# A mixture of experts behind a long convolution: routed gate and up products counted in half feature tiles

## The chip, the cores and the metric

The kernel runs on one core of a Trainium2 chip. The metric is the time of one execution on the device in microseconds (us). A core has TensorE (PE: matmuls, with its weight loads shown apart as PEld), VectorE (DVE), ScalarE (ACT), GpSimd (POOL), the SyncE queue (SP) that issues transfers, and 16 DMA engines.

## The reference

128 sequences with 32 heads of 512 features each (4096 rows of 512, called tokens here) go through a causal long convolution with a per-head kernel, are cut to each sequence's length, and then pass a mixture of experts; the result is added to the input.

```
y = irfft(rfft(x, 1024) * rfft(K, 1024))[..., :512] + x * D
y = y * (arange(512) < length[:, None])[:, None, :]     # lengths from 78 to 453

scores = sigmoid(y @ gate_w.T) + bias                   # 16 experts
w, idx = top_k(scores, 4);  w = w / sum(w)
for each expert e:   g = y @ Wg[e].T;  u = y @ Wu[e].T  # 512 -> 256
                     out += (w[e] * silu(g) * u) @ Wd[e].T
out += silu(y @ Sg.T) * (y @ Su.T) @ Sd.T               # shared expert
return x + out
```

What matters here: behind a sequence's length, features are zero. A token of a sequence of length 200 needs only its first 200 features in the products with gate_w, Wg and Wu.

## The kernel before

All data are float32. The work has three stretches. In the first (to about 145 us) TensorE convolves head by head (`convolve`, L515 to L535): matmuls against a strip of shifted kernels, then transposes that also sort the sequences by falling length, so that features stand on partitions and tokens on columns (`yT`, in the large tile `store`). Features are reversed, so that the zero features of short sequences come first: a token that needs n tiles of 128 features uses the last n of KT = 4. Convolved rows also go to a buffer in device memory, `y_rows`, with their routing weights behind them.

In the second stretch (about 145 to 298 us) `unit_step` computes the shared expert for 8 units of 16 sequences, while `slots` plans the routed work in steps between them. Each expert's tokens, sorted by falling length, fill tiles of 128 slots; the plan holds for each tile its expert (`texp`), the place of its weights in a ring (`woff`), the number of feature tiles that its longest token needs (`ntk`, 1 to 4, from the flags `reach` at L464), the rows to fetch (`get`) and the rows to add to (`put`).

The third stretch (about 298 to 925 us) goes over the routed tiles in an order written out by hand. `turn_of(step)` (L1121) is one turn of a software pipeline over three tiles at once; instructions keep this order on each engine:

- `gather(step + 4)`: GpSimd fetches the rows of a later tile into `yg`.
- `tokens(step)` (L1016): TensorE transposes the needed feature tiles (L1022, PSUM tile `m`), ScalarE copies them to `yt` (L1028), DVE picks each token's weight (L1029).
- `turn(step - 2)` (L1070): TensorE transposes the hidden values `zt` of an older tile in two halves (L1072, PSUM tile `u`), DVE copies them to `zT` (L1075).
- `inner(step - 1)` (L1050): for each needed feature tile one product of 128 rows with 512 columns, gates in the first 256 columns and ups in the rest, into one PSUM bank `g` (L1054). Then ScalarE's Silu (L1065) and DVE's product with the ups and the weight (L1066) make `zt`.
- `outer(step - 2)` (L1077): two products of 512 columns give the output (L1080, PSUM tile `o`); DVE copies it to `ob` (L1089), GpSimd adds it to the rows in device memory (L1090).
- `registers(step + 1)` (L1044): TensorE's instruction stream loads two values of the plan, the weights' place and the number of feature tiles (L1045, L1048).
- SyncE loads an expert's weights into the ring when the tile begins a new expert (L1139 to L1146).

The number of feature tiles is known only on the chip. `by_tiles` (L901) therefore compiles four versions of a piece of code and chooses by two comparisons on TensorE's stream. It is used for the transposes (L1027), for `inner` (L1063) and for the shared expert's products (L937).

The ring has R = 8 places of WSZ = 3072 columns (gates and ups 2048, down 1024; 1.5 MB each) and is loaded R - 1 experts ahead. It lies over `yT`, which the units release one after the other (`free_after`, L964). The last turns (L1153 on) each first ask for a flag whether there is such a tile.

Of the kernel before, what the change touches and what calls it, by code (L numbers as in the profile page):

```python
# [31 lines left out]
I32 = mybir.dt.int32  # L32
# [8 lines left out]
E, TOPK, I = 16, 4, 256  # L41
KT = L // P
IT = I // P
HB = 4
# [7 lines left out]
YW = L + E  # L52
R = 8
SPARE = 16
# [4 lines left out]
QC = P // KT  # L59
WSZ = 2 * KT * I + IT * L  # L60

# [14 lines left out]
def ssm_moe_kernel(  # L76
# [41 lines left out]
    for j in range(2):  # L118
# [19 lines left out]

    store = big.tile([P, 3 * WSZ + KT * H * P], F32, tag="store", name="store")
    yT = store[:, 2 * WSZ : 2 * WSZ + KT * H * P].rearrange(  # L140
        "p (u k h b) -> p u k h b", u=NU, k=KT, h=H
    )
    w_sh = store[:, 2 * WSZ + KT * H * P :]
    ring_flat = store[:, : R * WSZ]
    y_rows = d1.tile([B * H, YW], F32, tag="y_rows", name="y_rows")
# [73 lines left out]
    less = const.tile([E, P], BF16, tag="less", name="less")  # L219
    nc.gpsimd.memset(less, -float(KT - 1))  # L220

# [241 lines left out]

    reach = const.tile([P, KT], BF16, tag="reach", name="reach")  # L464
    nc.vector.memset(reach, 1.0)
    for n in range(1, KT):
        nc.vector.tensor_scalar(
            reach[:, n : n + 1], by_rank[:, 1:2], float(n * P), None, ALU.is_gt
        )
# [174 lines left out]
    def slots():  # L644
# [6 lines left out]

        pe = ps_m.tile([E, KT], F32, tag="m", name="pe")
        nc.tensor.matmul(pe, lhsT=cnt, rhs=reach, start=True, stop=True)
        many = ctile("many", [E, KT])
        nc.vector.tensor_copy(many, pe)
# [21 lines left out]
        t_e = tpos[:E, :]  # L677
        marks = ctile("marks", [E, KT + 1, NT], BF16)
        upto_n = ctile("upto_n", [E, KT - 1])
        nc.vector.tensor_scalar(  # L680
            upto_n, many[:, 1:], 1.0 / P, tstart, ALU.mult, ALU.add
        )
        nc.vector.tensor_scalar(marks[:, 0, :], t_e, tend, None, ALU.is_ge)
        nc.vector.tensor_scalar(marks[:, KT, :], t_e, tstart, None, ALU.is_lt)
        for n in range(1, KT):
            nc.vector.tensor_scalar(
                marks[:, n, :], t_e, upto_n[:, n - 1 : n], None, ALU.is_lt
            )
# [8 lines left out]
        nc.tensor.matmul(pr[:, 1, :], lhsT=used_b, rhs=marks[:, 0, :], start=True, stop=True)  # L697
        for n in range(1, KT):
            nc.tensor.matmul(
                pr[:, 2, :], lhsT=ones[:E, :], rhs=marks[:, n, :], start=(n == 1), stop=False  # L700
            )
        nc.tensor.matmul(pr[:, 2, :], lhsT=less, rhs=marks[:, KT, :], start=False, stop=True)
        rows3 = ctile("rows3", [P, 3, NT])
# [46 lines left out]
        def mod_r(dst, src, add):  # L750
# [8 lines left out]
        place, first = trow("place"), trow("first")  # L759
        woff, loff, load = trow("woff", I32), trow("loff", I32), trow("load", I32)  # L760
        mod_r(place, num[:1, :], 0)
        nc.vector.tensor_scalar(woff, place, float(WSZ), None, ALU.mult)
        mod_r(place, num[:1, :], R - 1)
        nc.vector.tensor_scalar(loff, place, float(WSZ), None, ALU.mult)
# [10 lines left out]
        made.update(  # L775
            texp=texp, woff=woff, load=load, loff=loff, lexp=lexp, lexp0=lexp0, ntk=ntk, fresh=fresh, full=full
        )
# [67 lines left out]
    xb = load_xt(0)  # L845
    nc.sync.dma_start(out=w_sh, in_=w_all[E])

# [52 lines left out]

    def by_tiles(k_t, some):  # L901


        with tc.If(k_t > 2) as many:
            with tc.If(k_t > 3) as all4:
                some(4)
            with all4.Else():
                some(3)
        with many.Else():
            with tc.If(k_t > 1) as two:  # L910
                some(2)
            with two.Else():
                some(1)

# [49 lines left out]
    def free_after(j):  # L964

        return min((max(j - 1, 0) * WSZ - 1) // (KT * TU), NU - 1)

# [3 lines left out]
    def unit_step(u):  # L971
# [3 lines left out]
        if u < NU:  # L975
            k_us[u] = nc.tensor.value_load(k_u[0:1, u : u + 1], min_val=1, max_val=KT)
            for it in range(IT):
                up(u, it, p_g, 0)
                if u == 0 and it == 0:
                    sums(NB - 1)  # L980
                    route(NB // RB - 1)
                nc.scalar.activation(sgu[it], p_g[it], AF.Silu)
                up(u, it, p_u, I)
                nc.vector.tensor_mul(at(zu, u)[:, it, :], sgu[it], p_u[it])
                if u > 0 or it > 0:
                    next(making, None)
# [15 lines left out]

    w0s, k_ts = {}, {}

    yt = homes(gp, "yt", [P, KT, P], 2)
    wts = homes(gp, "wt", [P, 1], 4)
    junks = homes(gp, "junk", [P, E], 2)
    sgs = homes(gp, "sgt", [P, I], 2)
    zs = homes(gp, "zt", [P, I], 2)
    zts = homes(gp, "zT", [P, IT, P], 2)  # L1010
    p_t, p_gu = homes(ps_m, "m", [P, KT, P], 2), homes(ps_g, "g", [P, 2 * I], 2)
    p_z = homes(ps_u, "u", [P, IT, P], 2)

    marks = {}

    def tokens(t):  # L1016
# [9 lines left out]
        else:  # L1026
            by_tiles(k_ts[t], transposes)  # L1027
        nc.scalar.copy(at(yt, t), pt)  # L1028
        nc.vector.scalar_tensor_tensor(  # L1029
            at(junks, t),  # L1030
# [7 lines left out]

    def in_ring(t, mm):
        for other in loads[t + 1 :]:  # L1040
            tc.declare_no_dep(mm.ins, other.ins, reason="another place of the ring")
        dep(mm, loads[t], "the tile's expert")

    def registers(t):  # L1044
        w0s[t] = nc.tensor.value_load(  # L1045
            made["woff"][0:1, t : t + 1], min_val=0, max_val=(R - 1) * WSZ
        )
        k_ts[t] = nc.tensor.value_load(made["ntk"][0:1, t : t + 1], min_val=1, max_val=KT)  # L1048

    def inner(t):  # L1050
        pgu = at(p_gu, t)
        def products(n):
            for q in range(KT - n, KT):
                mm = nc.tensor.matmul(  # L1054
                    pgu,
                    lhsT=at(yt, t)[:, q, :],
                    rhs=ring_flat[:, bass.ds(w0s[t] + q * 2 * I, 2 * I)],
                    start=(q == KT - n),
                    stop=(q == KT - 1),
                )  # L1060
                in_ring(t, mm)

        by_tiles(k_ts[t], products)  # L1063
        sg = at(sgs, t)
        nc.scalar.activation(sg, pgu[:, :I], AF.Silu)  # L1065
        nc.vector.scalar_tensor_tensor(  # L1066
            at(zs, t), pgu[:, I:], at(wts, t), sg, ALU.mult, ALU.mult
        )

    def turn(t):  # L1070
        for it in range(IT):
            nc.tensor.transpose(  # L1072
                at(p_z, t)[:, it, :], at(zs, t)[:, it * P : (it + 1) * P], ident
            )
        nc.vector.tensor_copy(at(zts, t), at(p_z, t))  # L1075

# [90 lines left out]
def _laid_out(inputs):  # L1167
# [9 lines left out]
    )  # L1177
    wgu = np.concatenate([wg, wu], axis=3).reshape(rows, P, KT * 2 * I)
    wd = wd.reshape(rows, L, IT, P).transpose(0, 3, 2, 1).reshape(rows, P, IT * L)
    laid = {  # L1180
# [10 lines left out]
        "bias": a["L0_ffn_bias"],  # L1191
        "w_all": np.concatenate([wgu, wd], axis=2),
    }
# [22 lines left out]
```

## Time and profile before

| what | value |
|---|---|
| runs of the kernel | 941.65, 943.94, 944.29 us; median 943.94 |
| the profiled execution: its time, its span | 942.44 us, 940.7 us |
| granted clock of TensorE over the span | 0.994 |
| stretch of the routed tiles, 298 to 923 us | 625.0 us, PE busy 621.6, DVE 222.2, ACT 130.3, POOL 343.1 |
| L1054, gate and up products | 742 records, busy 343.0 us |
| L1080, down products | 536 records, busy 252.2 us |
| L1022 and L1072, transposes | 373 and 268 records, busy 63.1 and 51.2 us |
| L1028, copy of the transposes (ACT, 128x512) | 136 of 586 ns |
| L1065, Silu (ACT, 128x256) | 135 of 384 ns |
| L1066, product to zt (DVE, 128x256) | 135 of 484 ns |
| L1075, copy to zT (DVE, 128x256) | 134 of 420 ns |

A group's row gives line, engine and operation, what it writes and reads, the count, then busy time in us and the mean length of one in ns, then the idle time of the engine just before such instructions, and what ended it. TensorE's matmuls overlap: the length of one runs from its start to its modelled end, and the next begins before that. What a matmul takes from the engine is read from the distances between starts. A float32 matmul appears as two records, each with its own weight load. A row of the timeline gives start and length in us, engine, line, operation, tiles and count. The view of one source line gives count and shortest/median/longest ns; an engine's name with a q stands for its instruction stream (register loads, branches, waits), which is not counted as busy. A row of busy times by stretch gives the stretch, its length, then busy time and number of instructions of PE, PEld, DVE, ACT and POOL, the granted clock, the busy share of the DMA engines and GB/s.

### The profile page before, as it was taken

What the parts mean: (1) busy time and instruction counts of PE and PEld (TensorE: products, weight loads), DVE (VectorE), ACT (ScalarE), POOL (GpSimd) and SP (SyncE); (2) the same over time, 40 slices, a digit from 0 to 9 for tenths busy, and PEclk for the clock granted to TensorE, in tenths of its full rate; (3) what the DMA queues carried; (4) which work ended last, traced back from release to release, by engine and by line L of the source; (5) the groups of instructions that cost most, each with busy time, mean ns of one, the idle gap of its engine ahead of it and who ended that gap; (6) DMA issues with size and microseconds to landing.
All of it is one profiled execution on the core that took longest, in us unless ns stands there. A gap on an engine that the chain in (4) does not pass through costs nothing.

```text
span 940.7 us, 14509 instructions
## 1 busy us (share of the span) xinstructions
PE 883.1 (94%) x2960; PEld 442.0 (47%) x2960; DVE 409.3 (44%) x1406; ACT 190.0 (20%) x375; POOL 422.7 (45%) x376
## 2 busy tenths in 40 slices
PE   0799997999999999999999999999999999999993
PEld 0455553444544444454444444444444444444441
DVE  7954555486950233433343334333433233344331
ACT  0122221111222122211222122212211111222220
POOL 4210000222456455655565456645655545566553
PEclk9999999999999999999999999999999999999997
DMA  4378873276769756776577567756766556667664
GB/s 163 108 253 290 293 275 137 30 249 132 184 96 233 198 111 115 138 170 116 110 135 181 114 115 126 130 101 110 134 113 114 100 106 109 109 130 138 118 114 83
DMA packets 54673, 135.95 MB, mean 145 GB/s; under 512 B 12400, under 2 KB 12560, under 8 KB 50960
## 3 DMA queue, kind: packets, MB, share of 16 engines
q0 software_dynamic: 36256, 89.77, 50.6%
q1 hardware_dynamic: 14064, 36.15, 11.3%
q10 hardware_dynamic: 4224, 8.39, 2.3%
q8 instruction: 71, 1.16, 0.5%
q14 instruction: 58, 0.48, 0.1%
HBM read 288.08 MB, written 60.64 MB: 371 GB/s over the span
## 4 chain that ended last, share of the span: by engine, by line
PE 66%; issue 1%; SPq 0%; POOL 0%; DVE 0%; ACT 0%; POOLq 0%
PE g L1054 34%; PE o L1080 24%; PE m L1022 4%; PE u L1072 3%; PE o L944 1%; POOL out L1090 0%; SPq L1157 0%; POOL yg L894 0%; SPq L1105 0%; SPq L1140 0%; SPq L1141 0%; DVE zt L1066 0%; SPq L1142 0%; ACT sgt L1065 0%; SPq L880 0%
## 5 line engine op out<-in xcount | busy, mean ns | idle before, releaser
L1054 PE MATMUL g<-store,yt 128*128 x742 | 343.0, 596 | 1.8 <-issue 1.5
L1090 POOL DMA_INDIRECT out<-ob,put x134 | 211.3, 1577 | 242.6 <-DVE junk L1029 214.4
L1080 PE MATMUL o<-store,zT 128*128 x536 | 252.2, 593 | 0.1
L1066 DVE SCALAR_TENSOR_TENSOR zt<-g,wt,sgt 128x256 f32<-128x256 f32 x135 | 65.3, 484 | 306.7 <-ACT sgt L1065 306.7
L1054 PEld LDWEIGHTS g<-store,yt 128*128 128x128 f32 x742 | 130.3, 190 | 118.7 <-issue 117.4
L1080 PEld LDWEIGHTS o<-store,zT 128*128 128x128 f32 x536 | 101.4, 190 | 129.3 <-issue 124.6
L894 POOL DMA_INDIRECT yg<-y_rows,get x140 | 138.1, 987 | 42.7 <-issue 31.7
L1089 DVE COPY ob<-o 128x512 f32<-128x512 f32 x134 | 92.7, 692 | 109.7 <-PE o L1080 101.6
L1028 ACT COPY yt<-m 128x512 f32<-128x512 f32 x136 | 79.7, 586 | 227.7 <-PE m L1022 219.3
L1065 ACT ACTIVATE sgt<-g 128x256 f32<-128x256 f32 x135 | 51.9, 384 | 268.2 <-PE g L1054 267.4
L953 POOL DMA_INDIRECT out<-ob,unit_rows x32 | 50.2, 1568 | 98.8 <-ACT ob L951 93.1
L520 PE MATMUL py<-strip,xt 128*128 128x512 f32 (+3 forms) x256 | 79.0, 447 | 7.9 <-DMA strip<-kd 7.9
L1022 PEld LDWEIGHTS m<-ident,yg 128*128 128x128 f32 x373 | 48.6, 141 | 73.1 <-issue 73.0
L1022 PE MATMUL m<-ident,yg 128*128 128x128 f32 x373 | 63.1, 273 | 1.3 <-issue 1.0
L944 PE MATMUL o<-store,z 128*128 128x512 f32 x128 | 57.7, 597 | 1.2 <-ACT yt L1028 1.2
L1075 DVE COPY zT<-u 128x256 f32<-128x256 f32 x134 | 56.3, 420 | 0.7 <-PE u L1072 0.7
L520 PEld LDWEIGHTS py<-strip,xt 128*128 128x128 f32 x256 | 42.5, 195 | 25.3 <-issue 12.3
L1072 PE MATMUL u<-ident,zt 128*128 128x128 f32 x268 | 51.2, 273 | 0.6 <-DVE zt L1066 0.6
L929 PE MATMUL g<-store 128*128 128x512 f32 x92 | 43.0, 602 | 3.1 <-issue 2.5
L865 POOL DMA_DIRECT2D out<-in_x x8 | 4.4, 558 | 88.3 <-ACT store L531 88.3
L929 PE MATMUL u<-store 128*128 128x512 f32 x92 | 42.2, 593 | 0.0
L809 DVE TENSOR_SCALAR cols<-tpos_h,stl,tok 128x143 f16<-128x143 f16 x128 | 41.8, 331 | 0.0
(272 smaller groups left out, 499.0 us busy)
## 6 DMA issues: line engine op xcount, KB each, us to landing
store<-in_w_all SPq DMA_DIRECT2D x143, 1536.0 KB
xt<-in_x_t SPq DMA_DIRECT2D x8, 1024.0 KB
y_rows<-yb ACTq DMA_DIRECT2D x8, 1024.0 KB
out<-in_x POOLq DMA_DIRECT2D x8, 1024.0 KB, 9.0
strip<-kd SPq DMA_DIRECT2D x7, 1024.0 KB
yg<-y_rows,get POOLq DMA_INDIRECT x140, 4.3
out<-ob,put POOLq DMA_INDIRECT x134, 4.8
strip<-kd SPq DMA_DIRECT2D x4, 256.0 KB
```

Source lines behind the costliest of these rows:

```text
L520: nc.tensor.matmul(py[:, : L - jt * P], lhsT=xt[:, jt, q, :], rhs=strip[tb][:, q, jt * P :], start=(jt == 0), stop=(jt == KT - 1),)
L894: nc.gpsimd.indirect_dma_start(out=at(yg, t), out_offset=None, in_=y_rows[:, :], in_offset=bass.IndirectOffsetOnAxis(ap=made["get"][:, t : ...
L929: nc.tensor.matmul(ps[it], lhsT=w_sh[:, c0 : c0 + P], rhs=yT[:, u, kt, :, :].rearrange("p h b -> p (h b)"), start=(kt == KT - n), stop=(kt ...
L944: nc.tensor.matmul(po, lhsT=at(zu, u)[:, it, q * P : (q + 1) * P], rhs=w_sh[:, c0 : c0 + L], start=(it == 0), stop=(it == IT - 1),)
L1022: nc.tensor.transpose(pt[:, q, :], at(yg, t)[:, q * P : (q + 1) * P], ident)
L1028: nc.scalar.copy(at(yt, t), pt)
L1054: mm = nc.tensor.matmul(pgu, lhsT=at(yt, t)[:, q, :], rhs=ring_flat[:, bass.ds(w0s[t] + q * 2 * I, 2 * I)], start=(q == KT - n), stop=(q = ...
L1066: nc.vector.scalar_tensor_tensor(at(zs, t), pgu[:, I:], at(wts, t), sg, ALU.mult, ALU.mult)
L1072: nc.tensor.transpose(at(p_z, t)[:, it, :], at(zs, t)[:, it * P : (it + 1) * P], ident)
L1080: mm = nc.tensor.matmul(po, lhsT=at(zts, t)[:, it, :], rhs=ring_flat[:, bass.ds(w0s[t] + WD + it * L, L)], start=(it == 0), stop=(it == IT ...
L1089: nc.vector.tensor_copy(ob, po)
L1090: add = nc.gpsimd.indirect_dma_start(out=out, out_offset=bass.IndirectOffsetOnAxis(ap=made["put"][:, t : t + 1], axis=0), in_=ob, in_offse ...
```

## The change

Need is counted in half feature tiles of HF = 64: `ntk` and `k_u` now run to MT = 8. `inner` chooses among eight versions instead of four. Gates and ups get a PSUM bank each (`gates_z` and `ups`), and every product with 512 columns becomes two with 256. For an odd number of halves, the feature tile of which only one half is needed goes first, as two products over 64 rows each: gates on TensorE's rows 64 to 127 (where `yt` has the half's features), ups on rows 0 to 63. For that, ScalarE copies the transposes' upper half a second time, to the lower partitions (`yt_up`), and the weights of the half (ups below, gates above) from the ring into `wx`, for every tile, at an offset that it loads into a register. The host lays out these halves behind each expert's weights; a place of the ring grows to 4096 columns (2 MB) and the ring shrinks to six places. The hidden values' transposes go into the gates' bank; `sgt` and `zt` are replaced by halves of the units' tile `sg`.

```diff
-R = 8
+R = 6
...
-WSZ = 2 * KT * I + IT * L
+WSH = 2 * KT * I + IT * L
+WSZ = WSH + KT * I
+Y0 = 2 * WSH
+X0 = Y0 + KT * H * P + WSH - R * WSZ
...
-    reach = const.tile([P, KT], BF16, tag="reach", name="reach")
+    reach = const.tile([P, MT], BF16, tag="reach", name="reach")
...
-    for n in range(1, KT):
+    for n in range(1, MT):
         nc.vector.tensor_scalar(
-            reach[:, n : n + 1], by_rank[:, 1:2], float(n * P), None, ALU.is_gt
+            reach[:, n : n + 1], by_rank[:, 1:2], float(n * HF), None, ALU.is_gt
         )
...
+        nc.vector.tensor_scalar(half_at, rows3[:1, 2, :], -1.0, float(MT - 1), ALU.mult, ALU.add)
+        floor_div(half_at, half_at, 2)
+        nc.vector.tensor_scalar(half_at, half_at, float(I), float(WSH), ALU.mult, ALU.add)
+        nc.vector.scalar_tensor_tensor(
+            xoff, place, float(WSZ), half_at, ALU.mult, ALU.add
+        )
...
+    def by_number(m, lo, hi, some):
+        if lo == hi:
+            some(lo)
+            return
+        mid = (lo + hi) // 2
+        with tc.If(m > mid) as more:
+            by_number(m, mid + 1, hi, some)
+        with more.Else():
+            by_number(m, lo, mid, some)
...
-        return min((max(j - 1, 0) * WSZ - 1) // (KT * TU), NU - 1)
+        return min((X0 + (j + 1) * WSZ - Y0 - 1) // (KT * TU), NU - 1)
...
         nc.scalar.copy(at(yt, t), pt)
+        nc.scalar.copy(at(yt_up, t), pt[HF:])
+        x0 = nc.scalar.value_load(
+            made["xoff"][0:1, t : t + 1], min_val=WSH, max_val=R * WSZ - I
+        )
+        in_ring(t, nc.scalar.copy(at(wx, t), ring_flat[:, bass.ds(x0, I)]))
...
     def inner(t):
-        pgu = at(p_gu, t)
-        def products(n):
-            for q in range(KT - n, KT):
-                mm = nc.tensor.matmul(
-                    pgu,
-                    lhsT=at(yt, t)[:, q, :],
-                    rhs=ring_flat[:, bass.ds(w0s[t] + q * 2 * I, 2 * I)],
-                    start=(q == KT - n),
-                    stop=(q == KT - 1),
-                )
-                in_ring(t, mm)
-
-        by_tiles(k_ts[t], products)
+        pg, pu = at(gates_z, t)[:, 0, :], at(ups, t)[:, 0, :]
+
+        def products(m):
+            n = (m + 1) // 2
+            if m % 2 == 1:
+                q = KT - n
+                for ps, rows, lhs in ((pg, slice(HF, P), at(yt, t)), (pu, slice(0, HF), at(yt_up, t))):
+                    nc.tensor.matmul(
+                        ps, lhsT=lhs[rows, q, :], rhs=at(wx, t)[rows, :], start=True, stop=(n == 1)
+                    )
+            for q in range(KT - m // 2, KT):
+                for ps, c0 in ((pg, 0), (pu, I)):
+                    mm = nc.tensor.matmul(
+                        ps,
+                        lhsT=at(yt, t)[:, q, :],
+                        rhs=ring_flat[:, bass.ds(w0s[t] + q * 2 * I + c0, I)],
+                        start=(q == KT - n),
+                        stop=(q == KT - 1),
+                    )
+                    in_ring(t, mm)
+
+        by_number(m_ts[t], 1, MT, products)
...
     def turn(t):
+        pz = at(gates_z, t)[:, 1, :].rearrange("p (i s) -> p i s", i=IT)
         for it in range(IT):
-            nc.tensor.transpose(
-                at(p_z, t)[:, it, :], at(zs, t)[:, it * P : (it + 1) * P], ident
-            )
-        nc.vector.tensor_copy(at(zts, t), at(p_z, t))
+            nc.tensor.transpose(pz[:, it, :], at(zs, t)[:, it * P : (it + 1) * P], ident)
+        nc.vector.tensor_copy(at(zts, t), pz)
```

## The prediction

> **What bounds the kernel now.** I read the engine shares, then the chain that ended last, then the groups of its two largest lines. The span is 940.7 us.
>
> ```profile
> PE 883.1 (94%) x2960; PEld 442.0 (47%) x2960; DVE 409.3 (44%) x1406; ACT 190.0 (20%) x375; POOL 422.7 (45%) x376
> ...
> L1054 PE MATMUL g<-store,yt 128*128 x742 | 343.0, 596 | 1.8 <-issue 1.5
> ...
> L1080 PE MATMUL o<-store,zT 128*128 x536 | 252.2, 593 | 0.1
> ```
>
> TensorE carries the chain (gate and up products 34%, down products 24%), and its two big groups hardly idle. The mean of 596 ns is a latency. The cost is the distance from start to start: the timeline of TensorE puts float32 matmuls over 512 columns 0.429 us apart, and each product is two such records (742 records are 371 products), so a product of one feature tile costs 0.858 us. In the convolution (L520), 256 columns are 0.216 apart and 128 columns 0.108, with the weight load hidden.
>
> "Busy" hides a second bound. Busy time by stretch, for five tiles of three feature tiles, five of two and three of four (span, then busy time of PE, PEld, DVE, ACT, POOL):
>
> ```profile
> 340.87:365.03 24.16, 24.16 (x77) 11.96 (x76) 8.28 (x26) 4.88 (x11) 12.81 (x10) 1.00 0.61 113
> 373.60:393.30 19.70, 19.65 (x61) 9.51 (x60) 8.14 (x26) 4.85 (x10) 12.84 (x10) 1.00 0.75 136
> 410.20:427.40 17.20, 17.20 (x54) 8.44 (x53) 4.87 (x16) 2.91 (x6) 7.69 (x6) 1.00 0.72 181
> ```
>
> A tile takes 4.83, 3.94 and 5.73 us. Counting starts, TensorE needs for n feature tiles 0.858n + 1.716 (down) + 0.108n (input transposes) + 0.216 (two z transposes): 4.83 for three, 3.86 for two, 2.90 for one. So tiles of three and four are bound by the array; tiles of two lose 0.08 us to something else. The timeline of one such tile shows it:
>
> ```profile
> 385.55 1.88 PE L1054 MATMUL g<-store,yt 128*128 x4
> 387.27 1.88 PE L1080 MATMUL o<-store,zT 128*128 x4
> 388.99 0.38 PE L1022 MATMUL m<-ident,yg 128*128 128x128 f32 x2
> 389.21 0.38 PE L1072 MATMUL u<-ident,zt 128*128 128x128 f32 x2
> 389.50 0.67 PE L1054 MATMUL g<-store,yt 128*128 x1
> ```
>
> The last line starts 0.07 late, as its weights were issued late. That is TensorE's own instruction stream: it waits for the zT copy (DVE, ends 386.50), issues the down products, loads two registers, branches, issues the transposes, branches again, and reaches the next gate product at 389.46, 2.97 us after zT. From the last z transpose (385.45) to zT's end is 1.05, so the loop is 4.0 less the 0.1 from that transpose to the gate product, 3.94, with the array at 3.86. Its parts:
>
> ```profile
> L1045 PEldq TENSOR_LOAD <-woff x137: 296/305/713, 286.8 to 923.8; - x137
> ...
> L905 PEldq COMPARE_BRANCH  x364: 65/179/400, 146.2 to 905.6; - x182
> ```
>
> A branch not taken is near 0.07, one taken near 0.21.
>
> **How many tiles are concerned.** I routed the reference's inputs by hand (scores, top 4, each expert's tokens by falling length, 128 to a tile). Tiles by half feature tiles m of the longest token: m=2: 8, 3: 21, 4: 23, 5: 28, 6: 26, 7: 28, together 134. By feature tiles this is 8, 44, 54, 28, which the trace confirms (9, 44, 54, 28 runs of 2, 4, 6, 8 records on L1054; the ninth is an empty tile). So 77 tiles are odd and use the pair; 56 of them (m of 5 and 7) are bound by the array.
>
> **The pair itself.** An odd tile's last product of 0.858 us becomes two 64-row products over 256 columns, gates on the upper rows, ups on the lower. Do they overlap? The gates' matmuls on 32 columns of the array (L551) do:
>
> ```profile
> 80.46 1.06 PE L551 MATMUL parts<-store,gw 128*32 128x512 f32 x8
> 81.45 0.33 PE L530 MATMUL pt<-to_rank,yb 128*128 128x128 f32 x1
> ```
>
> Eight records take 0.90 us, two after each other and four side by side. So the pair's four records should take 2 x 0.215 = 0.43. But the way in and out costs. The 16-row matmuls of the planning show it:
>
> ```profile
> 184.41 1.02 PE L944 MATMUL o<-store,z 128*128 128x512 f32 x2
> 185.37 0.23 PE L739 MATMUL pl<-marks,ones 16*128 16x143 bf16 x1
> 185.44 0.17 PE L740 MATMUL pl<-marks,ones 16*128 16x7 bf16 x1
> 185.53 1.13 PE L929 MATMUL g<-store 128*128 128x512 f32 x2
> ```
>
> The second L944 record starts at 184.84 and streams until 185.27; the next weight load begins 0.09 later. After the last small matmul (a few ns of columns) the next load begins 0.095 later, in the same 2 ns as its matmul, so it isn't hidden: that matmul is recorded with 697 ns instead of 592, 0.105 for the load. **Here the Trainium skill's rule speaks against the change**: "TensorEngine Tiling (Array Packing)", Key Properties, says that changing the tiling mode drains TensorE, without a price. "TensorE: Matmul & The Clock Gate", Part 3 (the span model), prices packed matmuls at one duration plus 4 ns per further tile. By the span model alone an odd tile saves 0.858 - 0.43 = 0.42, 77 x 0.42 = 33 us in all. By the rows, each pair pays two drains (0.19) and two exposed loads (0.21): 0.43 + 0.40 = 0.83, a saving of 0.03. I take the rows: both ways of dividing the array show about 0.095 on each side. Float32 halves over 64 rows are not in this trace; from both sides, 0.42 saved (no switch seen) to 0.40 lost (no overlap: 0.86 + 0.40). On the 56 array-bound tiles my value gives -1.6 us.
>
> **The split.** Every full product is now two of 256 columns on two banks: four records of 0.2155 for two of 0.429, +0.004, times 294 left: +1.2. Weights are loaded twice (190 ns each) behind matmuls of 215; the convolution's 256-column form shows that this fits. Without this cover it would be 0.1 per record.
>
> **TensorE's instruction stream.** Inner products choose among eight cases instead of four: one branch more, +0.13 (not taken) or +0.27 (taken, odd m). Against this, in the compiled order the first gate product no longer waits for ScalarE beside the load, which frees the separate semaphore instruction (0.05, 0.125 with what lies around it), and the pair needs no address registers (0.11). Net about 0 for m=4, +0.03 for m=3. The additional address instructions for ups (0.13 each) lie before the zT wait and are hidden behind it. The stream's rows grow from 7,778 to 15,764. Instructions arrive in 16 KB packets (71 on q8 in the span, one per 2.7 tiles); shortly before such a packet a branch takes some 0.12 more (0.29 to 0.33 at 345.5, 358.2, 388.8). With about one packet per tile that is +0.08. Tiles of m=3 and 4 have no slack for it: 44 x 0.1 = **+4.4**, bounded by 0 and by 0.35 each (15) if packets arrive late. Tiles of m of 5 and more have 0.4 us of slack here (branches end 343.85, zt arrives at 344.55).
>
> **ScalarE.** Per tile it gets the second copy of the transposes (64x512; by L1028's 586 ns, since columns count), a register load (L1157's on this engine: 0.275 to 0.887, median 0.35, plus 0.3 for its two register operations), and the copy of the weights (128x256; 0.38 by L1065). All stand ahead of the tile before's Silu:
>
> ```profile
> 385.59 0.59 ACT L1028 COPY yt<-m 128x512 f32<-128x512 f32 x1 [1.61 <-PE m L1022]
> 387.47 0.38 ACT L1065 ACTIVATE sgt<-g 128x256 f32<-128x256 f32 x1 [1.30 <-PE g L1054]
> ```
>
> From 385.59: copy to 386.18, second copy to 386.83, the load and its operations beside it until about 387.1, weights to 387.5, Silu at 387.6. For m=4 that is 0.1 late, and z (ends 388.38) has 0.3 to spare before the stream asks for it (388.69): nothing. For m of 5 and more the products end later than that: nothing. For m=2 the products end 0.86 earlier, and Silu, z and the next gate products hang on ScalarE: about 3.8 us instead of 3.3, 8 x 0.5 = **+4**, between 0 and 6.
>
> **The rest.** Planning gets four more marks with their matmuls, four reach columns and the half offsets, some fifteen small DVE operations on the start and on the units' stretch, which TensorE fills: +1 (0 to 2). The ring has 6 places instead of 8, each load 2 MB instead of 1.5: at five experts ahead and most experts over 20 tiles long, hidden; if not, one wait of some 10 us. Moving the ring frees its places by other units, still before the first tile.
>
> Sum: 1.2 - 1.6 + 4.4 + 4 + 1 = +9 on the profiled execution's 942.4, 951.4; the median of the runs is 1.5 above that execution, so **953**.
>
> **Rivals.**
> *Not slower:* the pair's weights load while the array drains. Place: the 56 array-bound odd tiles. With both loads hidden a pair costs 0.62 and saves 0.24, 13 us, against +10.6 of the rest: 941; with no switch cost at all 0.42, 930. It decides from 0.19 saved per tile. For it: the two loads can run side by side. Against it: both rows above show the load only after the drain. 15%.
> *ScalarE becomes the gate:* register load at its longest (0.887), copies not overlapping. Silu is then some 0.65 late on all 52 tiles up to m=4, of which 0.3 is slack: +0.35 x 52 less the 4 counted, 967. For it: 20% busy says nothing of order in a queue. 15%.
> *The halves don't overlap:* +0.43 on 56 and 0.35 on 21: +31, 984. Against it: L551. 8%.
> *No change:* packets stay hidden and m=2 tiles hold their slack: 944. 12%.
> *Forecast*, 947 to 962: 50%.
>
> Three thousandths (2.8 us) is what can be told from no change here. Faster 0.15, the same 0.12, slower 0.73. The range 938 to 984 leaves out the deepest gain and combined losses.
>
> **What would show it.** Right: pairs with starts a few ns apart, 0.83 us from the z transpose's end to the first full product, array-bound odd tiles as long as before, tiles of m=3 and 4 above 4.0 us. Wrong: odd tiles of m=5 under 4.6 us (the rival that isn't slower), Silu's idle time ended by its own engine on m=4, or TensorE waiting for the load.

## The result, and the profile after

| | before | after |
|---|---|---|
| median of the runs, compared on one chip | 942.80 us (940.97 to 944.29, 4 runs) | 969.82 us (969.17 to 971.99, 4 runs) |
| profiled execution, span | 940.7 us | 967.5 us |
| granted clock of TensorE over the span | 0.994 | 0.993 |

The changed kernel takes 1.0288 times as long (95% interval 1.0268 to 1.0308): 27 us more. The forecast was about 10 more (953).

From the page of the kernel before, the queue that brings instructions and the head of the chain of work that ended last:

```profile
q8 instruction: 71, 1.16, 0.5%
...
PE 66%; issue 1%; SPq 0%; POOL 0%; DVE 0%; ACT 0%; POOLq 0%
```

From the page of the changed kernel: the engine shares, the queue that brings instructions, the head of the chain, and the groups of the products and of the pair (the two halves of an odd feature tile).

```profile
PE 892.5 (92%) x3706; PEld 549.7 (57%) x3706; DVE 412.2 (43%) x1420; ACT 311.4 (32%) x647; POOL 422.7 (44%) x376
...
q8 instruction: 149, 2.44, 1.0%
...
PE 75%; issue 9%; DVE 6%; POOL 4%; DMA 4%; ACT 0%; SPq 0%; POOLq 0%; DVEq 0%; ACTq 0%
...
L1099 PE MATMUL g<-store,yt 128*128 x586 | 185.1, 398 | 7.7 <-issue 7.4
...
L1099 PE MATMUL u<-store,yt 128*128 x586 | 174.3, 379 | 0.0
...
L1094 PE MATMUL g<-wx,yt 64*128 64x256 f32 x156 | 54.3, 428 | 8.9 <-issue 8.0
```

"Issue" has grown from 1% of the chain to 9%. It is time in which TensorE waited for nothing that the trace shows. It stands before the first product of a tile: 7.4 us where that is a full product, 8.0 where it is the pair; before, the same place had 1.5. Another 4.6 us stand before the input transposes (L1056), where it was 1.0. The instruction queue q8 brings 149 packets instead of 71. Over the tiles no row names ScalarE or a load of the ring as what TensorE waited for.

Three stretches show where the time went. They hold the same tiles in both kernels: five tiles of five and six halves near the start; eight of three and four halves in the middle; three of five halves near the end. Columns: stretch, length, busy time of PE, PEld, DVE, ACT, POOL, clock, DMA share, GB/s. Before:

```profile
336.03:360.23 24.20, 24.20 (x77) 12.00 (x76) 8.31 (x26) 4.86 (x10) 12.81 (x10) 1.00 0.60 113
470.76:502.63 31.87, 31.65 (x100) 15.52 (x99) 13.52 (x41) 7.76 (x16) 20.52 (x16) 1.00 0.73 136
799.46:813.98 14.52, 14.52 (x47) 7.20 (x46) 4.99 (x16) 2.91 (x6) 7.69 (x6) 1.00 0.60 110
```

After:

```profile
339.55:367.97 28.42, 26.22 (x105) 16.50 (x106) 8.70 (x26) 9.28 (x21) 13.04 (x11) 1.00 0.59 109
483.39:516.86 33.47, 32.31 (x132) 19.70 (x130) 14.30 (x44) 15.61 (x34) 20.78 (x17) 1.00 0.74 135
818.80:833.25 14.45, 14.45 (x64) 9.31 (x63) 4.98 (x16) 5.57 (x13) 7.69 (x6) 1.00 0.63 115
```

The clock is the same, and the DMA engines carry as much. In the third stretch the array is never idle, and a tile takes 4.82 us where it took 4.84: the change costs nothing there, and gains next to nothing. In the second, TensorE is idle for 1.16 us (33.47 less 32.31) where it was for 0.22, and a tile takes 4.18 instead of 3.98. In the first, 2.20 us are idle and a tile takes 5.68 instead of 4.84.

Over all tiles, by halves m of the longest token (from the distances of the tiles' first product starts):

| m | tiles | us per tile, before to after | change of the sum, us |
|---|---|---|---|
| 2 | 8 | 3.67 to 3.99 | +2.6 |
| 3 | 21 | 3.98 to 4.32 | +7.2 |
| 4 | 23 | 3.97 to 4.33 | +8.4 |
| 5 | 28 | 4.82 to 4.91 (median 4.82) | +2.3 |
| 6 | 26 | 4.84 to 5.02 (median 4.86) | +4.6 |
| 7 | 28 | 5.73 to 5.70 | -0.9 |

These changes sum to 24.1. With 2.7 us before the first product, that is the whole 26.9 by which the profiled execution is late at the end of the tiles. The 2.7 are not the tiles' and not the plan's: in the stretch of the units the profile of the changed kernel has 3.4 us at half clock. Before, then after, for the same 3.6 us:

```profile
205.60:209.20 3.60, 3.60 (x10) 1.67 (x9) 0.88 (x5) 0.60 (x1) 0.25 (x1) 1.00 1.06 377
205.60:209.20 3.60, 3.60 (x6) 1.37 (x5) 1.30 (x7) 0.00 (x0) 0.00 (x0) 0.53 1.05 248
```

Other profiles have such pieces there too (e1 and e6, with the plan of before, and e4, e5, e9, e10 and e12), and all of these reach the first product 2 to 4.5 us late; those without one (e2, e3, e7, e8, e11) are within 0.9 us of the kernel before. Why the clock falls there no run shows. It makes whole executions differ by a few us (e11 takes 942.6 us at a granted clock of 0.995, 948.8 at 0.989), so the experiments are also read on the tiles alone. Tiles of m = 4 and 6 have no pair, and lose no less than their odd neighbours.

The pair itself did what its two rows had said. TensorE's timeline at an ordinary tile of the changed kernel (start, length, instruction, count, idle time before it):

```profile
499.46 0.38 PE L1116 MATMUL g<-ident,sg 128*128 128x128 f32 x2
500.03 0.48 PE L1094 MATMUL g<-wx,yt 64*128 64x256 f32 x1 [0.18 <-issue]
500.03 0.48 PE L1094 MATMUL u<-wx,store 64*128 64x256 f32 x1
500.35 0.38 PE L1094 MATMUL g<-wx,yt 64*128 64x256 f32 x1
500.35 0.38 PE L1094 MATMUL u<-wx,store 64*128 64x256 f32 x1
500.66 0.70 PE L1099 MATMUL g<-store,yt 128*128 x2
```

The gates' and the ups' matmul start together (7 ns apart in the records) and run side by side. The second two follow 0.32 later: 0.215 of columns and 0.105 of a weight load that nothing hides. The first full product starts 0.31 after that: 0.215 of columns and a gap of 0.095, which the prediction reads as the array's drain; its own load is again exposed (its second record, in the same row, starts at 500.98, 0.32 later instead of 0.215). The same gap stands on the way in where nothing else delays the pair (0.093 at 818.70 us). So the float32 pair takes two times 0.215, and a gap and an exposed load on its way in and on its way out, and replaces 0.858 us by nearly as much.

The loss is in the 0.18 ahead of the pair, and at other tiles in more. TensorE's timeline further on, with the same steps:

```profile
606.29 0.38 PE L1056 MATMUL m<-ident,yg 128*128 128x128 f32 x2
606.51 0.38 PE L1116 MATMUL g<-ident,sg 128*128 128x128 f32 x2
607.75 0.48 PE L1094 MATMUL g<-wx,yt 64*128 64x256 f32 x1 [0.86 <-issue]
```

All operands are there, yet the pair starts 0.86 us late. Line 919 chooses among the versions of the products. The view of that line on TensorE's instruction stream over the whole execution (count, shortest/median/longest ns):

```profile
L919 PEldq COMPARE_BRANCH  x539: 65/176/1588, 298.3 to 950.1; - x180
```

The same view from 602.7 to 608.3 us alone, the stretch of the timeline above:

```profile
L919 PEldq COMPARE_BRANCH  x6: 70/192/1362, 602.7 to 608.1; - x6
```

One branch in that window took 1.362 us, where a taken one takes some 0.21. Before, the longest branch over the tiles (L905) took 0.356:

```profile
L905 PEldq COMPARE_BRANCH  x322: 65/179/356, 298.0 to 905.6; - x161
```

In the changed kernel 61 branches of L919 take more than 0.4 us, all of them ahead of the products, and what they take above 0.3 each comes to 18.8 us. Of the 44 tiles of m = 3 and 4, 26 have such a branch: it is the jump past the longer versions to the short ones that lie behind them.

The first of the three stretches lost most, and there no branch of L919 is late. Late is the first register load, which stands behind the down products and not at a jump. That load before (L1045, five tiles), then the load and the branches after:

```profile
L1045 PEldq TENSOR_LOAD <-woff x5: 299/303/309, 337.0 to 356.4; - x5
...
L1079 PEldq TENSOR_LOAD <-woff x5: 571/628/922, 342.2 to 364.5; - x5
...
L919 PEldq COMPARE_BRANCH  x20: 65/176/214, 340.2 to 367.7; - x20
```

The loads are longer, and the stream also stands still for 1.0 to 1.5 us ahead of each of the five, where the usual distance is 0.08. Why the loads themselves are longer stays open. The standstill can be set against the packets of q8 in the trace: each of the five loads starts 1.3 to 1.5 us after the end of a packet. Of the 61 late branches, 25 end 1.3 to 1.6 us after one and none sooner than 1.24, while only 34 of the other 475 branches of L919 end in that interval. So the records agree with a wait for code that has just been brought. The turns are written out one after the other (a Python loop around `turn_of`), so longer code in a turn is code that must be brought anew every turn.

### The profile page after: what moved, and what is told of

The parts are those of the page before. It is cut to its first block, busy times and chain, and to the rows that moved or that the text cites. A ratio compares the mean times of both kernels' runs of the same rounds, so it can differ in the third digit from the quotient of the medians.

```text
span 967.5 us, 17467 instructions
## 1 busy us (share of the span) xinstructions
PE 892.5 (92%) x3706; PEld 549.7 (57%) x3706; DVE 412.2 (43%) x1420; ACT 311.4 (32%) x647; POOL 422.7 (44%) x376
## 4 chain that ended last, share of the span: by engine, by line
PE 75%; issue 9%; DVE 6%; POOL 4%; DMA 4%; ACT 0%; SPq 0%; POOLq 0%; DVEq 0%; ACTq 0%
PE o L1122 24%; PE g L1099 15%; PE u L1099 13%; PE g L1094 5%; PE m L1056 4%; POOL out L978 3%; PE g L1116 3%; PE py L524 3%; DMA strip<-kd 3%; PE g L954 2%; PE u L954 1%; PE o L969 1%; DMA out<-ob,unit_rows 1%; PE pt L534 1%; DVE yb L531 1%
## 5 line engine op out<-in xcount | busy, mean ns | idle before, releaser
L1099 PE MATMUL g<-store,yt 128*128 x586 | 185.1, 398 | 7.7 <-issue 7.4
L1111 DVE SCALAR_TENSOR_TENSOR sg<-u,wt,sg 128x256 f32<-128x256 f32 x135 | 65.3, 484 | 282.0 <-ACT sg L1110 279.5
L1099 PE MATMUL u<-store,yt 128*128 x586 | 174.3, 379 | 0.0
L1099 PEld LDWEIGHTS g<-store,yt 128*128 128x128 f32 x586 | 100.4, 189 | 47.6 <-issue 39.1
L1099 PEld LDWEIGHTS u<-store,yt 128*128 128x128 f32 x586 | 111.3, 190 | 15.1
L1056 PEld LDWEIGHTS m<-ident,yg 128*128 128x128 f32 x373 | 47.9, 141 | 80.4 <-issue 79.3
L1110 ACT ACTIVATE sg<-g 128x256 f32<-128x256 f32 x135 | 51.9, 384 | 113.4 <-issue 55.4
L1063 ACT COPY store<-m 64x512 f32<-64x512 f32 x136 | 79.2, 582 | 3.3
L1056 PE MATMUL m<-ident,yg 128*128 128x128 f32 x373 | 63.8, 275 | 4.7 <-issue 4.6
L1094 PE MATMUL g<-wx,yt 64*128 64x256 f32 x156 | 54.3, 428 | 8.9 <-issue 8.0
L1117 DVE COPY zT<-g 128x256 f32<-128x256 f32 x134 | 56.3, 420 | 3.1 <-PE g L1116 2.8
L1067 ACT COPY wx<-store 128x256 f32 x136 | 54.8, 403 | 0.5 <-ACT store L1063 0.2
```

The costliest lines, as they stand in the source:

```text
L1056: nc.tensor.transpose(pt[:, q, :], at(yg, t)[:, q * P : (q + 1) * P], ident)
L1063: nc.scalar.copy(at(yt_up, t), pt[HF:])
L1094: nc.tensor.matmul(ps, lhsT=lhs[rows, q, :], rhs=at(wx, t)[rows, :], start=True, stop=(n == 1))
L1099: mm = nc.tensor.matmul(ps, lhsT=at(yt, t)[:, q, :], rhs=ring_flat[:, bass.ds(w0s[t] + q * 2 * I + c0, I)], start=(q == KT - n), stop=(q = ...
```

## Experiments

Three theories stand in the expectations in one form or another. **Fetch** (F): TensorE's code has grown so long that the instructions behind a jump aren't there when it lands. **ScalarE** (S): its three added operations per tile make Silu late, and with it z and the next products. And the **pair** or the **split** themselves cost more than was worked out. All medians are compared with the kernel before on the same chip (942.6 to 942.7 us). "On the tiles" is the profiled execution's time from the first product of the first tile to that of the last, against before (625.6 us).

### ScalarE's work alone (e1_scalar_added)

The kernel before, and in the tile's copies:

```diff
         nc.scalar.copy(at(yt, t), pt)
+        nc.scalar.copy(at(yt_up, t)[:64], pt[64:])
+        x0 = nc.scalar.value_load(
+            made["woff"][0:1, t : t + 1], min_val=0, max_val=(R - 1) * WSZ
+        )
+        in_ring(t, nc.scalar.copy(at(wx, t), ring_flat[:, bass.ds(x0, I)]))
```

To make room, `sgt` and `zt` are halves of the units' tiles, as in the change.

> The kernel before, plus what ScalarE got: second copy of the transposes (64x512), a register load, a copy of 128x256 weights out of the ring, all ahead of Silu. Nothing reads the copies; TensorE's program stays as it is. Theory F (TensorE's instruction stream: more code, packets that come late on long jumps): 0 to +3 us, 942 to 946. Theory S (ScalarE is the gate, Silu late): +10 to +20 us, tiles of two feature tiles above 4.2 us. Theory P (the pair on half the rows costs more than it saves): no change.

943.96 us, 1.0012 (1.0003 to 1.0021): 1.3 us. Its Silu group:

```profile
L1071 ACT ACTIVATE sg<-g 128x256 f32<-128x256 f32 x135 | 51.9, 384 | 155.6 <-PE g L1060 155.2
```

ScalarE is idle for 155.6 us before the 135 Silus, and the gate products end 155.2 of them. So Silu still waits for TensorE, behind all of the added work. On the tiles e1 loses 1.3 us, and its tiles of m = 2 nothing (3.66 us, before 3.67). Theory S falls.

The prediction's own sign for this rival, Silu's idle time ended by ScalarE itself, does stand in the changed kernel's row (and the view of the line gives 71 times for it):

```profile
L1110 ACT ACTIVATE sg<-g 128x256 f32<-128x256 f32 x135 | 51.9, 384 | 113.4 <-issue 55.4 <-ACT wx L1067 49.0 <-PE g L1099 7.5
...
  ACT wx L1067: 49.0, 71
```

But that idle time comes after the copy's end, 0.69 us on average, so the copy isn't what Silu waits for. e11 below has nearly the same row (46.8) and is within 0.5 us of before on the tiles.

### The split alone (e6_split_only)

The kernel before with gates and ups in a bank each and every product as two of 256 columns, still in four versions.

```diff
-                mm = nc.tensor.matmul(pgu, ...)
+                for ps, c0 in ((pg, 0), (pu, I)):
+                    mm = nc.tensor.matmul(ps, ...)
```

> The kernel before with gates and ups in two banks and every product split into two of 256 columns; four versions, no halves, no pair. Theory F: 943 to 949, as the program grows to 10,640 rows, with the array paying 0.004 us per product (1.5 us) and Silu starting earlier. If the split itself were dear (weights loaded twice): above 955.

943.58 us, 1.001 (1.0001 to 1.002): 1.0 us, against 1.2 in the sum, and 1.2 on the tiles. The weights loaded twice stay hidden. q8 brings 96 packets here, and there is hardly a loss from them (six branches above 0.4 us).

### Code that never runs (e2_dead_small, e3_dead_large)

The kernel before, with one more comparison ahead of the choice, which is never true, as no tile has more than four feature tiles. The two differ only in how much code lies behind it: one product, or 28.

```diff
-        by_tiles(k_ts[t], products)
+        with tc.If(k_ts[t] > KT) as never:
+            for _ in range(1):        # e3: range(7)
+                products(1)           # e3: products(4)
+        with never.Else():
+            by_tiles(k_ts[t], products)
```

> The kernel before, plus one never taken alternative ahead of the inner products, with a single product in it: one more branch taken per tile (about 0.28 us of TensorE's stream), almost no code. Theory F: the 44 loop-bound tiles pay the branch, +8 to +13 us, no branch far above 0.33. Theories S and P: the same, as this is the control of the next run.

> As the run before, with 28 products in the never taken alternative, so that TensorE's program has as many rows as the changed kernel's (16,073; the changed kernel 15,764). The same instructions are executed as in the control. Theory F: 10 to 25 us slower than the control, with branches of 0.4 to 1.4 us at the jump. Theories S and P: within 2 us of the control.

With one product 951.50 us, 1.0098 (1.008 to 1.0117); with 28 products 973.54, 1.033 (1.0311 to 1.0349). The same instructions run in both, and the distance is 22 us. The added branch in e2, past the small piece of code (view of line 1063):

```profile
L1063 PEldq COMPARE_BRANCH  x135: 202/208/343, 294.4 to 930.1; - x135
```

The same branch in e3, past the large one:

```profile
L1063 PEldq COMPARE_BRANCH  x135: 207/347/1742, 294.1 to 949.3; - x135
```

It is always taken, and costs 0.208 when the jump is short. Past the long piece the median is 0.347 and the longest 1.742, and 63 of 135 take over 0.4. q8 brings 75 and 146 packets. That code which never runs costs 22 us shows the core of theory F: it is the length of the code, not what is run of it. Both runs have the plan and the ring of before, so the larger loads of the changed ring aren't needed for the loss.

The small one has a reading of its own: a taken branch more on every tile cost 8.9 us (8.2 on the tiles), mostly on tiles of m = 2 to 4, which went from 3.98 to 4.10 (m = 3) and 3.97 to 4.12 (m = 4). These tiles are bound by TensorE's instruction stream, as the prediction said.

### Fewer or shorter versions (e4_no_pair, e5_six_versions)

e4 is the changed kernel without the pair and without ScalarE's three operations, still with eight versions: an odd tile's last feature tile is a whole product. e5 is the changed kernel with six versions, as no tile has one half or eight.

```diff
-            for q in range(KT - m // 2, KT):
+            for q in range(KT - n, KT):       # e4, and the pair's lines gone
...
-        by_number(m_ts[t], 1, MT, products)
+        by_number(m_ts[t], 2, MT - 1, products)   # e5
```

> The changed kernel without the pair: odd versions compute the whole feature tile over 128 rows, and ScalarE's second copy, register load and weight copy are gone; eight versions of the code, the split in 256 columns, the plan and the ring stay. Theory F: nothing won, 968 to 980 (each odd version now has more code). Theory S: 946 to 952. Theory P: 955 to 962.

> The changed kernel with the versions for 1 and 8 halves left out (the lengths are 78 to 453, so they never serve a tile): the pair, ScalarE's work, plan and ring stay, TensorE's program falls from 15,764 rows to 12,905, and some tiles pay a branch less. Theory F: most of the loss on the routed tiles goes, 948 to 960. If only the number of branches counted: 23 tiles of four halves and 28 of seven save 0.07 to 0.13, 965 to 969.

e4: 980.82 us, 1.0425 (1.0387 to 1.0463), the slowest of all, just above the 968 to 980 expected. Without the pair the code is longer (16,909 instructions of TensorE's program against 15,764, 153 packets), and tiles of m = 3 and 4 take 4.53 and 4.52. The pair, then, is not the cause. e5: 950.65 us, 1.0072 (1.0044 to 1.0101): two versions that no tile uses cost 19 us (18.6 on the tiles). It has 12,905 instructions, 122 packets, and 31 branches above 0.4 us instead of 61; tiles of m = 3 and 4 are back at 4.13 and 4.11, and those of m = 5 and 7 gain (4.80 and 5.67, before 4.82 and 5.73).

### The pair in short code (e9_compact, e11_compact_whole)

e9 has three versions by the number of whole feature tiles, with the pair as a choice inside each; products behind the first are shared. e11 is as short, but without the pair: odd tiles are computed whole, in four versions, and the split, the plan, the ring and ScalarE's work stay as in the change.

```diff
-        by_number(m_ts[t], 1, MT, products)
+        def products(f):                               # e9
+            with tc.If(m_ts[t] > 2 * f) as odd:
+                halves(KT - f - 1)
+                whole(f, [KT - f], True)
+            with odd.Else():
+                whole(f, [KT - f], False)
+            whole(f, range(KT - f + 1, KT), False)
...
+        by_tiles(m_ts[t], products)                    # e11
```

> The changed kernel with the same products in less code: versions for 1 to 3 whole feature tiles, the pair and the first whole tile inside them behind a test for odd, the rest shared; 11,618 rows on TensorE instead of 15,764. Pair, ScalarE's work, plan and ring stay. Theory F: below the kernel with six versions (12,905 rows, 950.7): 944 to 951. If size had nothing to do with it: 965 to 970.

> The changed kernel with four versions by whole feature tiles and no pair (odd tiles compute the whole tile); ScalarE's added work, split, plan and ring stay; 10,331 rows. Against the compact kernel with the pair it shows what the pair is worth once the code is small. By the pair's rows (0.03 us per array-bound odd tile, 56 of them): within 3 us of the compact kernel, 945 to 950. If the pair saved 0.24 us per tile as the rival had it: 10 us or more above the compact kernel.

e9: 948.66 us, 1.0055 (1.0039 to 1.0071), 11,618 instructions, 105 packets. The branches that choose among its versions take 0.434 at the longest. The view of the first of their lines:

```profile
L1113 PEldq COMPARE_BRANCH  x189: 65/208/434, 298.2 to 928.9; - x189
```

e11: 945.11 us, 1.0027 (1.0016 to 1.0037), 10,331 instructions, 96 packets. On the tiles e11 is only 0.5 us slower than before, with the loads, the plan and ScalarE's work of the change. So e4 and e11 both compute odd tiles whole, and stand 36 us apart, by 6,578 instructions of code and a comparison more per tile, although e11 has ScalarE's work and e4 hasn't. The pair's own worth is read from e9 against e11: tiles of m = 5 and 7 are 4.80 and 5.66 with it, 4.84 and 5.73 without: 0.04 to 0.07 saved each, some 3 us over 56 tiles. But tiles of m = 3 and 4 are 4.03 and 4.12 with it and 3.99 and 3.97 without, since its choice is a branch more on them. With the pair the kernel is 3.5 us slower (2.5 on the tiles), even where hardly a branch is late. Within 3 us had been expected, from the odd tiles' saving alone; what the choice costs was left out.

### Moving the register load, turning the jump (e7, e8, e10, e12)

If the instruction stream binds short tiles, a register load ahead of the wait for zT should be hidden. In the turn's order:

```diff
+            registers(step + 1)
             if step >= 2:
                 outer(step - 2)
-            registers(step + 1)
```

(lines around it left out). e7 does this to the kernel before, e8 to the changed kernel, e10 to e9. e12 does it to the changed kernel too, and puts the short versions first, so that long tiles make the long jump:

```diff
-        with tc.If(m > mid) as more:
-            by_number(m, mid + 1, hi, some)
-        with more.Else():
-            by_number(m, lo, mid, some)
+        with tc.If(m < mid + 1) as less_:
+            by_number(m, lo, mid, some)
+        with less_.Else():
+            by_number(m, mid + 1, hi, some)
```

> The kernel before, with the two register loads of the next tile moved ahead of the down products, so that they run while TensorE's stream would wait for zT. The loop bound of the tiles of one and two feature tiles falls below the array's need: 3.86 instead of 3.95 us on 44 tiles, 936 to 941. If the stream is not what bounds these tiles: 942 to 944.

> The changed kernel with the same move of the register loads. Theory F with the loop: stalls at the long jumps have about 1.2 us more of cover, so tiles of three and four halves fall from 4.3 to about 3.9 us: 948 to 957. If the array or ScalarE bound them: 968 to 971.

> The same with the register loads ahead of the down products. Theory F with the loop: 3 to 5 us below the compact kernel, 939 to 947. Where a pair is worth more than switching costs it would beat the kernel before with this move alone (940.4); by the rows of the pair it should not.

> The changed kernel with the eight versions in rising order, so that tiles of up to four halves jump past the long versions behind their products and not ahead of them; same program size. Theory F: the late packet is then met while the stream would wait for zT anyway, at least in part: 952 to 964, with the long branches at the end of the versions. If place does not matter: 967 to 972.

e7: **940.42 us**, 0.9978 (0.9971 to 0.9985), the fastest kernel here, below both. The eight tiles of m = 3 and 4 of the second stretch above, in e7:

```profile
470.96:502.24 31.28, 31.28 (x100) 15.22 (x99) 13.53 (x41) 7.74 (x16) 20.51 (x16) 1.00 0.78 136
```

31.28 us instead of 31.87, and TensorE is never idle in it: 3.91 per tile, where the array needs 3.86. The gain of 2.2 us in the median is under the three thousandths that the prediction set as its bound, but the interval lies clear of 1, and on the tiles e7 gains 3.2.

e10: 945.39 us, 1.0022 (1.0011 to 1.0033), 3.3 under e9, as expected of it. On the tiles it is level with before (0.3 under), and 2.9 behind e7, which has the same move and no pair.

e8: 963.77 us, 1.0239 (1.0207 to 1.0271), a miss: 948 to 957 had been expected. It took 6 us off the changed kernel (4.4 on the tiles), not the bulk of the loss. The five tiles of the first stretch are back at 4.86, their loads no longer late. But the late branches stayed (66 above 0.4 us), and m = 4 still takes 4.45. The expectation had taken lateness for a fixed delay that cover can hide. e12: 972.42 us, 1.0321 (1.0299 to 1.0344), a miss too (952 to 964): some 50 late branches still stand ahead of products, most of them now in tiles of m of 5 and more, which make the long jump, and it is no faster than the changed kernel.

So neither cover ahead of the jump nor its direction mends it, only less code. By packets of q8, all runs in line, with the median and the change on the tiles:

| packets | 71 | 71 | 72 | 75 | 96 | 96 | 105 | 105 | 122 | 146 | 149 | 149 | 149 | 153 |
|---|---|---|---|---|---|---|---|---|---|---|---|---|---|---|
| us | 940.4 (e7) | 942.8 (before) | 944.0 (e1) | 951.5 (e2) | 943.6 (e6) | 945.1 (e11) | 948.7 (e9) | 945.4 (e10) | 950.7 (e5) | 973.5 (e3) | 969.8 (after) | 963.8 (e8) | 972.4 (e12) | 980.8 (e4) |
| on the tiles, us | -3.2 | 0 | +1.3 | +8.2 | +1.2 | +0.5 | +3.1 | -0.3 | +5.6 | +27.9 | +24.1 | +19.8 | +23.8 | +34.3 |

Up to 122 packets the times follow the branches and the work. From 146 on, about one packet per turn, every kernel is 21 us or more above before.

## Why the prediction was wrong, point by point

- **The bound.** Right. Tiles of two feature tiles (m = 3 and 4) hang on TensorE's instruction stream: a taken branch more slowed them (e2), a register load moved out of the way brought them to within 0.05 of the array (e7).
- **The pair.** Right. The halves overlap, and pay the gaps and the exposed loads. -0.02 us per tile on the three tiles of m = 5, 0.04 to 0.07 saved in e9 against e11, forecast 0.03. The Trainium skill's span model ("TensorE: Matmul & The Clock Gate", Part 3) would, as an estimate, have had 0.42 saved per odd tile; the measurement decides against it here.
- **The split.** Right: +1.2 in the sum, +1.0 in e6 (1.2 on the tiles), which has the whole of the split and the banks.
- **TensorE's instruction stream.** This is the step that failed: "With about one packet per tile that is +0.08. Tiles of m=3 and 4 have no slack for it: 44 x 0.1 = **+4.4**, bounded by 0 and by 0.35 each (15) if packets arrive late." Mechanism and tiles were right, the size was not. The 0.12 was read from branches of the kernel before, where a packet serves 2.4 tiles (55 packets over the 134; the prediction's 2.7 is a mean over the whole span) and the longest branch took 0.356. With a packet per tile the jump took 0.43 to 1.36 us in 26 of the 44 tiles of m = 3 and 4, and the 44 lost 0.35 each on average, 15.6 us: the end that the text had named and not taken.
- **"Tiles of m of 5 and more have 0.4 us of slack here."** Wrong by the same term: slack of 0.4 doesn't cover a delay of 1. Tiles of m = 5 and 6 lost 6.9 us (forecast: -0.8 by their pairs), 4.2 of it in the stretch of the five tiles above, where the stream stood still ahead of the register loads and not at the jump. Most others kept their time (medians 4.82 and 4.86). The 28 tiles of m = 7 gained 0.9.
- **ScalarE.** For m of 3 and more right: it costs next to nothing (e1: 1.3 on the tiles, nearly all of it on m = 3 and 4). For m = 2 the sum had +4, and +2.6 was measured, but that is luck. With the same work on ScalarE the tiles of m = 2 lost nothing in e1 (-0.1 in sum) and in e11 (-0.9). The term was wrong, and the 2.6 belong to the stream.
- **Planning and ring.** No row shows TensorE waiting for a load of the ring. That most experts are over 20 tiles long isn't so: by m along the tiles at least ten experts follow each other, and four of these runs are over 20 long; nothing came of it. Up to the first product the changed kernel is 2.7 us later, against +1, but that goes with the piece at half clock. Without one, e8 and e11 reach it 0.5 us before and 0.1 after the kernel before, with the plan and the ring of the change: the plan cost nothing that can be seen.
- **The rivals.** "Not slower" fell, as both loads show; ScalarE as the gate fell by e1 and e11; halves that don't overlap fell by the timeline. No change fell by the result. The sum stood at +9 and the profiled executions are 26.9 apart at the end of the tiles. Of the 18 missing, 11.2 are the stream on m = 3 and 4 (15.6 for 4.4), and 7.6 the tiles of m = 5 and more, which lost 6.0 where they were to gain 1.6; the other terms all but cancel.

What stays open is why fetch falls behind so steeply between 122 and 146 packets: whether the request for a packet goes out too late, the transfer waits for other traffic before it begins, or the jump discards what was brought. e8 and e12 rule out two simple forms of it. The transfer itself isn't slower (a packet of q8 takes 0.96 us in the median before and after), and the heavier ring isn't the reason: e3 loses 19.7 us on the tiles against e2 with the loads of before, and e11 loses 0.5 with the new ones. No run lightened the DMA traffic alone.

## What to carry to other kernels

Versions of a piece of code that are chosen on the chip have a price even when they don't run: count how many instructions a turn carries on each engine, and read the packets of the instruction queue per turn and the longest branch, not the median. A cost taken from the kernel before holds for its own rate: a packet every 2.4 tiles was hidden but for 0.12 us, a packet every tile was not. And where half of the work on a small tile is to be saved, put the switch of the array's division beside it, with its two gaps and two exposed loads: 0.83 us instead of 0.858 is hardly a gain, and one branch to choose it costs more.

## What the runs showed of the hardware

- Never-executed code in every turn slowed the kernel by 22 us (e3 against e2): branches past it took up to 1.74 us instead of 0.21.
- In the changed kernel 25 of 61 late branches end 1.3 to 1.6 us after the end of a 16 KB packet of q8. So do standstills of 1.0 to 1.5 us ahead of a register load that no jump leads to, in five tiles in a row.
- The loss sets in steeply: with 96 packets the tiles lose 1.2 us (e6), with 122 there are 31 late branches and 5.6 lost (e5), with 149, in the changed kernel, there are 61 and 24 lost.
- It isn't spread evenly. The five tiles of the first stretch lost 0.84 us each with the same code in which the three of the third lost nothing.
- Float32 matmuls on 64 rows of the array do run in pairs, their starts 7 ns apart, but the division costs a gap of 0.095 us and 0.105 for the weight load that it exposes, on the way in and on the way out.
- Pieces of 3.4 to 6.8 us at half clock stand in the units' stretch of some executions and not of others; the first product then comes 2 to 4.5 us later.
